# Gated experts on one Trainium2 core: the residual added into the accumulators at mid pass, and closing column products carried by ScalarE

## The chip, the cores and the metric

The kernel runs on one core of one Trainium2 chip. The metric is the device time of the whole program in microseconds, as the median of several runs. The profile is one further execution, taken by the hardware profiler; its span runs from the first to the last instruction. Engines are named TensorE (PE, its weight loads PEld), VectorE (DVE), ScalarE (ACT), GpSimd (POOL) and SyncE (SP, which issues nearly all DMAs; its queue is SPq).

## The reference

`x` is 8 blocks of 512 rows by 256 columns in fp32. Each block goes through eight experts and one shared expert. For an expert with weights Wg, Wu (256 x 1024) and Wd (1024 x 256):

```python
g = einsum('bsd,edf->ebsf', h, Wg)
u = einsum('bsd,edf->ebsf', h, Wu)
expert_outs = einsum('ebsf,efd->ebsd', silu(g) * u, Wd)
expert_output = einsum('be,ebsd->bsd', gating_probs, expert_outs)
shared = (silu(h @ Sg) * (h @ Su)) @ Sd
x = x + (1 - sg) * expert_output + sg * shared
```

The last line is the residual: the input `x` itself is added to the result. This sum is what the change moves.

## The kernel before

**Tiling.** The eight blocks are two halves of four (`h` = 0, 1, `NI` = 4). A half is worked through in 18 units: nine experts (the shared one is the ninth) times two groups of 512 of the 1024 hidden columns. Units are numbered 0 to 35; unit 17 is the last of the first half, unit 18 opens the second. In a unit, four blocks meet four weight tiles of 128 hidden columns. The kernel does not multiply each block with each tile in the plain way: it keeps combinations with the coefficients `CI` = (0, 1, -1, 2), which spares products. The four products of a block with its own tile make up the "hub" (P and Q steps), and the six pairs of blocks (`PAIRS`) follow, with differences and sums of inputs (`x_difference`, `x_sums`) and of weights (`w_difference`, `w_sums`). A pair has two steps R1 (a product of differences, L503) and four steps R (L513), for the gate (m = 0) and the up projection (m = 1). Gate results go through SiLU on ScalarE (L444), VectorE multiplies them with the up result and the expert's coefficient to h (L449).

**Down projection.** `down` (L550) is a generator of 26 steps, called "D": three for each of six pairs (r, then S or s, then a product with X at L618), four p steps with row sums and four q steps with column sums. The results are collected for the whole half in SBUF accumulators `acc["b", i]` and `acc["B", i]`, one of each for a block (and S and V for pairs). They are "turned": hidden direction across partitions, rows along the free direction. A step in `carried` (L584) first lets ScalarE copy the accumulator into a PSUM bank (L578), lets TensorE add its product there, and lets ScalarE copy the bank back (L587). A step with `single` (L592) starts an empty bank, and `put` adds it to the accumulator on VectorE (L566, L568, L570). The down projection uses two PSUM banks in turn. In the unit that closes a half (unit 17, and 34 for the second) S and V are also emptied into b and B, which adds VectorE operations.

**Order.** The main loop walks a written string of steps: "G" is a step of gate and up, "D" a step of down. A unit's D steps are late by eleven: the first eleven D of a unit finish the down projection of the unit before. TensorE and GpSimd keep the written order everywhere; ScalarE keeps it only in unit 0. VectorE, SyncE and, after unit 0, ScalarE are ordered by a planner, which takes what is ready by its own cost model, earlier written work first. Each engine executes its own order strictly.

**Turning back.** When the first half has closed, `turn_back` (L663) transposes each accumulator on VectorE (L669) in the D steps of unit 18, adds the residual (L670), which SyncE has loaded as 32-column squares of `x` (`load_back`, L659), and stores the result in four DMAs (L673). For the second half `end_step` transposes the accumulators (L689), writes them to DRAM, loads them back by rows (L707), and GpSimd adds them to rows of `x` (L711). Unit 35 itself multiplies straight into rows (`tail`, L720), and `store_rows` adds and stores (L729, L731).

**First unit.** In unit 0 the x differences and sums are computed (VectorE L288 and L302, ScalarE L290, GpSimd L303) and stored to DRAM; later units load them (L292 `v`, L309 `b`). The differences lie in a pool `v` of three buffers, the sums in a pool `b` of two.

Of the kernel before, what the change touches and what calls it, by code (L numbers as in the profile page):

```python
# [16 lines left out]
def kernel(  # L17
# [40 lines left out]
    P = 128  # L58
# [63 lines left out]
    back = {}  # L122
# [18 lines left out]
    def load_rows(pool, tag, b):  # L141
        rows = []
        for c in range(2):
            if pool is not xpool:
                t = pool.tile([P, 2, D], F32, tag=tag, name=f"xin{b}_{c}")
            elif c == 0:
                both = pool.tile([P, NT, D], F32, tag=tag, name=f"xin{b}")
            if pool is xpool:
                t = both[:, 2 * c : 2 * c + 2]
# [7 lines left out]
    def squares(a, b, q):  # L157

        return a[b].rearrange("s (k q d) -> q s k d", k=2, d=32)[q]
# [122 lines left out]
    def x_difference(u, p):  # L282

        i, j = PAIRS[p]
        v = vpool.tile([P, S], F32, tag="v", name=f"v{u.name}_{p}")
        if (u.h, p) not in scratch:
            d = CI[i] - CI[j]
            ve.tensor_sub(v, xhub[u.h, i][:, 0], xhub[u.h, j][:, 0])  # L288
# [261 lines left out]
    def down(u, acc):  # L550
# [81 lines left out]
        for what in (0, 1, 2, 3, 4, "p0", "q0", 5, "q1", "p1", "q2", "p2", "q3", "p3"):  # L632
# [7 lines left out]
            else:  # L640
                flush_sums(u, "cols", i)
                po, _ = single(("q", i), u.ad[i], u.cols[i])
                put(("B", i), po, 1.0)
                done[what] = po
# [6 lines left out]

    BACK = [(0, 1), (0, 0), (2, 1), (2, 0), (1, 1), (1, 0), (3, 1), (3, 0)]

    def load_back(h, i):

        if (h, i) not in back:
            xr = iopool.tile([P, S // 32, 2, 32], F32, tag="io", name=f"xr{h}_{i}")
            for q in range(4):
                nc.sync.dma_start(xr[ts(q, 32)], squares(x, NI * h + i, q))  # L659
            back[h, i] = xr  # L660
        return back[h, i]

    def turn_back(h, i, r):  # L663

        b = NI * h + i
        block = ends.pop((h, i, r))
        xr = load_back(h, i)
        t = zpool.tile([P, S], F32, tag="z", name=f"to{b}_{r}")
        ve.transpose(t, block)  # L669
        ve.tensor_add(xr[:, :, r], t.rearrange("p (c d) -> p c d", d=32), xr[:, :, r])  # L670
        if (i, 1 - r) not in BACK[BACK.index((i, r)):]:
            for q in range(4):
                nc.sync.dma_start(squares(out, b, q), xr[ts(q, 32)])  # L673
            if i in (0, 2):
                load_back(h, i + 1)
# [5 lines left out]
    end_stores = []  # L681

    def end_step(kind, i):

        b = NI * (NH - 1) + i
# [5 lines left out]
        elif kind == "store":  # L691
            to = end_rows[i] = dram.tile([S, D], F32, tag=f"end{i}", name=f"endrows{i}")
            at = to.rearrange("(c r t) d -> r t c d", r=32, t=NT)
            for r in range(2):
                for q in range(4):
                    end_stores.append((
# [3 lines left out]
        elif kind == "x":  # L700
            last_rows[i] = load_rows(xpool, "x", b)
        elif kind == "load":
            at = end_rows[i].rearrange("(p t) d -> p t d", t=NT)
            end_rows[i] = []
            for c in range(2):
                t = sumpool.tile([P, 2, D], F32, tag="sum", name=f"endin{i}_{c}")
                nc.sync.dma_start(t, at[:, 2 * c : 2 * c + 2])  # L707
                end_rows[i].append(t)
        else:
            for xr, t in zip(last_rows[i], end_rows[i]):  # L710
                gp.tensor_tensor(xr, xr, t, ALU.add)  # L711
# [13 lines left out]
    def store_rows(j, c):  # L725
        b = NI * (NH - 1) + j
        xr = last_rows[j][c]
# [12 lines left out]
    def gate_up(u, nxt):  # L740
# [19 lines left out]
        for kind, i, m in hub_steps(u):  # L760
# [6 lines left out]
            elif kind == "P":  # L767
                P_step(u, i, m)
                if u.n == 0 and m == 1 and i in (1, 3):
                    for p, make in ahead[:2] if i == 1 else ahead[2:]:  # L770
                        make(u, p)
# [8 lines left out]
        if u.n == 0:  # L780
            make_ad(u)
            for p in range(len(PAIRS)):
                d_forms(u, p)
        for p in range(len(PAIRS)):
# [13 lines left out]
            for m in range(2):  # L798
                if not last:
                    R1_step(u, p + 1, m)  # L800
                    if m == 0 and u.n == 0 and p and p + 1 < len(PAIRS):
                        sums(p + 1)
# [3 lines left out]
                for r in range(2):  # L806
                    R_step(u, p, m, r)
                    if m == 1 and r == 1:
# [3 lines left out]
                        if p + 2 < len(PAIRS) and u.n:  # L812
# [16 lines left out]
        7: (("turn", 0), ("store", 0)), 16: (("turn", 1), ("store", 1)), 18: (("x", 0),),  # L829
        20: (("turn", 2), ("store", 2), ("x", 1)), 22: (("load", 0), ("x", 2)),  # L830
        24: (("turn", 3), ("store", 3), ("x", 3)), 28: (("add", 0),), 30: (("load", 1),),
        34: (("add", 1),), 37: (("load", 2),), 40: (("add", 2),), 44: (("load", 3),),
        47: (("add", 3),),
# [7 lines left out]
    AHEAD_AT = (8, 11, 14, 17, 20)  # L841
    BACK_AT = (6,10,11,13,15,18,20,23)
# [22 lines left out]
    for u in units:  # L865
# [6 lines left out]
        for what in FIRST if u.n == 0 else LAST if nxt is None else ORDER:  # L872
            if what == "G":
                if nG == TAKE:
                    for _ in behind:
                        pass
                    if u.opens:
                        acc = {}
                    behind = down(u, acc) if nxt is not None else iter(())
# [24 lines left out]
            else:  # L904
# [54 lines left out]
```

## Time and profile before

| | |
|---|---|
| median of 3 runs | 2446.45 us (2445.05 to 2447.55) |
| the profiled execution | 2446.47 us |
| its span | 2444.7 us |
| TensorE busy | 2431.5 us, 99% |
| VectorE busy | 1928.9 us, 79% |
| ScalarE busy | 1239.4 us, 51% |
| GpSimd busy | 2080.0 us, 85% |
| granted TensorE clock, mean | 0.999 |
| DMA, mean | 106 GB/s |

A row of the profile gives line, engine and operation, what is written from what is read, sizes and count, then busy time and the mean duration in ns, then the idle time of the engine before such instructions and what ended it. In a timeline a row is a start and a duration in us, and in brackets the idle time before with its releaser. In a table by stretches each engine has its busy time in that stretch and the number of its instructions, followed by the granted TensorE clock, the DMA share and GB/s. One fp32 product of 128 x 128 by 512 columns is recorded as two matmul instructions.

### The profile page before, as it was taken

How to read it: one execution, taken by the hardware profiler on the slowest of the kernel's cores; microseconds unless marked ns; L12 is line 12 of the kernel's file. 1: busy time of each engine (PE TensorE's matmuls, PEld its weight loads, DVE VectorE, ACT ScalarE, POOL GpSimd, SP SyncE). 2: the span in 40 equal slices, each digit the busy share in tenths (PEclk: the TensorE clock that was granted, in tenths of full speed). 3: DMA queues.
4: the chain of work that ended last, by engine and by line, in shares of the span. 5: the costliest groups of instructions: out<-in, count | busy, mean ns of one | idle time of the engine just before them, and what ended most of it. 6: DMA issues, size and time to landing. Idle time of an engine off the chain costs nothing.

```text
span 2444.7 us, 22778 instructions
## 1 busy us (share of the span) xinstructions
PE 2431.5 (99%) x5736; PEld 1085.1 (44%) x5736; DVE 1928.9 (79%) x2870; ACT 1239.4 (51%) x2294; POOL 2080.0 (85%) x2313
## 2 busy tenths in 40 slices
PE   9999999999999999999999999999999999999999
PEld 4444444444444444444444444444444444444446
DVE  7778878777777877787987777777777777777795
ACT  5555554554555555555445555555555555555542
POOL 8988888898988989898878888888888888888872
PEclk9999999999999999999999999999999999999999
DMA  4333343343433333344353233323333333233245
GB/s 158 101 105 111 104 112 112 103 134 102 126 110 97 105 111 97 106 129 125 112 118 120 85 95 91 91 81 99 99 104 103 95 97 92 88 91 92 86 117 149
DMA packets 237841, 260.02 MB, mean 106 GB/s; under 512 B 80656, under 2 KB 173072, under 8 KB 237712
## 3 DMA queue, kind: packets, MB, share of 16 engines
q1 hardware_dynamic: 236880, 258.27, 35.9%
q8 instruction: 48, 0.79, 0.1%
q14 instruction: 81, 0.66, 0.1%
q10 hardware_dynamic: 832, 0.30, 0.0%
HBM read 240.69 MB, written 17.83 MB: 106 GB/s over the span
## 4 chain that ended last, share of the span: by engine, by line
PE 96%; POOL 1%; DVE 1%; DMA 1%; issue 0%; ACT 0%; SPq 0%; ACTq 0%; DVEq 0%; POOLq 0%
PE c L513 30%; PE c L503 15%; PE c L481 10%; PE c L458 10%; PE r L595 7%; PE r L618 7%; PE S L579 5%; PE b L579 5%; PE q L595 5%; PE s L595 2%; PE tail L720 1%; DMA sgt<-ondB_sharedgateprob_dram 0%; POOL wd L429 0%; POOL wb L396 0%; DVE h L449 0%
## 5 line engine op out<-in xcount | busy, mean ns | idle before, releaser
L513 PE MATMUL c<-b,wb 128*128 128x512 f32 x1728 | 848.1, 593 | 2.6 <-DMA b<-xs 1.9
L444 ACT ACTIVATE sg<-c 128x512 f32<-128x512 f32 x576 | 343.8, 597 | 595.0 <-DVE c L518 343.7
L449 DVE SCALAR_TENSOR_TENSOR h<-sg,coef,c 128x512 f32<-128x512 f32 x576 | 427.8, 743 | 235.6 <-PE c L513 128.3
L513 PEld LDWEIGHTS c<-b,wb 128*128 128x128 f32 x1728 | 328.3, 190 | 412.9 <-issue 390.0
L503 PE MATMUL c<-v,u 128*128 128x512 f32 x864 | 441.5, 593 | 1.9 <-ACT c L498 1.4
L540 POOL TENSOR_TENSOR rows<-rows,h 128x512 f32<-128x512 f32 x280 | 369.0, 1318 | 0.0
L508 DVE TENSOR_TENSOR c<-D,c 128x512 f32<-128x512 f32 x432 | 298.7, 692 | 81.1 <-ACT sg L444 61.4
L540 POOL TENSOR_TENSOR cols<-cols,h 128x512 f32<-128x512 f32 x280 | 357.7, 1277 | 0.0
L518 DVE TENSOR_TENSOR c<-c,D 128x512 f32<-128x512 f32 x432 | 298.6, 691 | 22.3 <-PE c L513 22.1
L396 POOL TENSOR_TENSOR wb<-u,wb 128x256 f32<-128x256 f32 x108 | 79.2, 733 | 237.3 <-ACT wb L394 237.3
L458 PE MATMUL c<-x,w 128*128 128x512 f32 x572 | 274.5, 592 | 0.0
L503 PEld LDWEIGHTS c<-v,u 128*128 128x128 f32 x864 | 163.0, 189 | 210.0 <-issue 163.9
L595 PE MATMUL r<-h,wd 128*128 128x512 f32 x420 | 215.4, 594 | 0.0
L618 PE MATMUL r<-X,ud 128*128 128x512 f32 x420 | 214.5, 592 | 0.0
L529 DVE TENSOR_TENSOR X<-h,h 128x512 f32<-128x512 f32 x210 | 206.1, 982 | 6.8
L481 PE MATMUL c<-x,at 128*128 128x512 f32 x432 | 209.4, 593 | 1.2 <-DVE P L474 0.7
L491 ACT COPY D<-c 128x512 f32<-128x512 f32 x284 | 165.8, 584 | 83.8 <-DVE h L449 83.8
L540 POOL TENSOR_TENSOR rows<-h,h 128x512 f32<-128x512 f32 x140 | 195.4, 1396 | 0.0
L540 POOL TENSOR_TENSOR cols<-h,h 128x512 f32<-128x512 f32 x140 | 181.0, 1293 | 0.0
L464 ACT COPY P<-c 128x512 f32<-128x512 f32 x216 | 126.6, 587 | 106.9 <-PE c L458 102.3
L458 PEld LDWEIGHTS c<-x,w 128*128 128x128 f32 x572 | 108.5, 190 | 135.9 <-issue 111.9
L578 ACT COPY S<-accS 128x512 f32<-128x512 f32 x132 | 77.9, 590 | 149.8 <-DVE accV L566 140.7
(108 smaller groups left out, 3472.5 us busy)
## 6 DMA issues: line engine op xcount, KB each, us to landing
b<-xs SPq DMA_DIRECT2D x210, 512.0 KB, 3.6
v<-xs SPq DMA_DIRECT2D x210, 256.0 KB, 2.6
wd<-in_L_cond_Wd_dram SPq DMA_DIRECT2D x32, 512.0 KB, 4.9
w<-in_L_cond_Wg_dram SPq DMA_DIRECT2D x127, 128.0 KB, 3.5
w<-in_L_cond_Wu_dram SPq DMA_DIRECT2D x127, 128.0 KB, 3.6
f<-xd SPq DMA_DIRECT2D x12, 512.0 KB, 3.6
xs<-f SPq DMA_DIRECT2D x18, 256.0 KB, 3.0
xin<-in_x_dram SPq DMA_DIRECT2D x16, 256.0 KB, 4.1
```

The lines of the kernel that those rows point to most:

```text
L444: nc.scalar.activation(s, bank, AF.Silu)
L449: ve.scalar_tensor_tensor(t, u.sg[i, j], coef[:, u.e, b : b + 1], bank, ALU.mult, ALU.mult)
L458: nc.tensor.matmul(bank, u.raw[i][:, m, 0], xhub[u.h, i][:, 0], start=True, stop=True)
L481: nc.tensor.matmul(bank, u.at[i][:, m], xhub[u.h, i][:, 1], start=False, stop=True, skip_group_check=True,)
L503: nc.tensor.matmul(bank, u.U[p][:, m], u.V[p], start=False, stop=True, skip_group_check=True)
L508: ve.tensor_sub(other, u.Ds[j, m], bank)
L513: nc.tensor.matmul(bank, u.W[p][:, r, m], u.VB[p][:, r], start=False, stop=True, skip_group_check=True,)
L518: ve.tensor_add(bank, bank, u.Ds[j, m])
L540: gp.tensor_tensor(sums[n], u.h_[n, n] if first else sums[n], u.h_[at], ALU.add)
L579: nc.tensor.matmul(po, w, b, start=not full, stop=True, skip_group_check=full)
L595: nc.tensor.matmul(po, w, b, start=True, stop=True)
L618: nc.tensor.matmul(A, u.Ud[p], u.X[p], start=False, stop=True, skip_group_check=True)
```

## The change

It has these parts.

1. **Residual at mid pass.** A new generator `residual` adds `x` to the accumulators `b` and `B` of the half on VectorE, with the coefficients that the turned combinations need. One operation is taken at each of the D steps 7, 13 and 19 of units 11 to 15 of a half. It reads the turned input tiles that lie in SBUF for the whole half.
2. **Turning back without a residual.** `turn_back` transposes straight into the output tile. The loads of `x` as squares (`load_back`) and the additions (L670) are gone. The four stores of a block are put into a list `outgoing`, and one is issued per G step. In the end of the second half the loads of `x` rows and GpSimd's additions are gone; rows of a block are loaded by one DMA into the x pool, and three of the four loads stand at G step 31, 38 and 45 where they stood at 30, 37 and 44.
3. **Closing q steps.** In a closing unit the q product is `carried`: copied in and out by ScalarE, where it was `single` with an addition on VectorE.
4. **First unit.** The x differences of pairs 3 and 4 lie in buffers of the pool `io` (two buffers, otherwise unused there). The sums of the second pair and the difference of the third are written after the hub, and the sums of a pair are made at the end of the pair two before it, as in the other units, where they were made one G step later.

```diff
     def x_difference(u, p):
 
         i, j = PAIRS[p]
-        v = vpool.tile([P, S], F32, tag="v", name=f"v{u.name}_{p}")
+        if u.n == 0 and p in (3, 4):
+            v = iopool.tile([P, 2, S], F32, tag="io", name=f"v{u.name}_{p}")[:, 0]
+        else:
+            v = vpool.tile([P, S], F32, tag="v", name=f"v{u.name}_{p}")
...
                 flush_sums(u, "cols", i)
-                po, _ = single(("q", i), u.ad[i], u.cols[i])
-                put(("B", i), po, 1.0)
-                done[what] = po
+                if closes(u):
+                    carried(("B", i), u.ad[i], u.cols[i])
+                else:
+                    po, _ = single(("q", i), u.ad[i], u.cols[i])
+                    put(("B", i), po, 1.0)
+                done[what] = True
...
+    def residual(acc, h):
+
+        for i in range(NI):
+            c, b, B = CI[i], acc["b", i], acc["B", i]
+            v, A = xhub[h, i][:, 0], xhub[h, i][:, 1]
+            for to, x_, s in ((b, v, 1.0), (b, A, c), (B, A, 1.0 + c * c), (B, v, c)):
+                if s == 1.0:
+                    ve.tensor_add(to, to, x_)
+                elif s == -1.0:
+                    ve.tensor_sub(to, to, x_)
+                elif s != 0.0:
+                    ve.scalar_tensor_tensor(to, x_, s, to, ALU.mult, ALU.add)
+                else:
+                    continue
+                yield
...
-    def turn_back(h, i, r):
-
-        b = NI * h + i
-        block = ends.pop((h, i, r))
-        xr = load_back(h, i)
-        t = zpool.tile([P, S], F32, tag="z", name=f"to{b}_{r}")
-        ve.transpose(t, block)
-        ve.tensor_add(xr[:, :, r], t.rearrange("p (c d) -> p c d", d=32), xr[:, :, r])
-        if (i, 1 - r) not in BACK[BACK.index((i, r)):]:
-            for q in range(4):
-                nc.sync.dma_start(squares(out, b, q), xr[ts(q, 32)])
-            if i in (0, 2):
-                load_back(h, i + 1)
+    def turn_back(h, i, r):
+
+        if i not in backs:
+            backs[i] = iopool.tile([P, S // 32, 2, 32], F32, tag="io", name=f"to{h}_{i}")
+        t = backs[i]
+        ve.transpose(t[:, :, r], ends.pop((h, i, r)).rearrange("p (c d) -> p c d", d=32))
+        if (i, 1 - r) not in BACK[BACK.index((i, r)):]:
+            del backs[i]
+            at = out[NI * h + i].rearrange("s (k q d) -> q s k d", k=2, d=32)
             for q in range(4):
+                outgoing.append((at[q], t[ts(q, 32)]))
...
-                    for p, make in ahead[:2] if i == 1 else ahead[2:]:
+                    for p, make in ahead[:2] if i == 1 else ahead[2:3]:
...
         if u.n == 0:
+            for p, make in ahead[3:]:
+                make(u, p)
             make_ad(u)
...
-                    if m == 0 and u.n == 0 and p and p + 1 < len(PAIRS):
-                        sums(p + 1)
...
-                        if p + 2 < len(PAIRS) and u.n:
+                        if p + 2 < len(PAIRS):
                             sums(p + 2)
...
-        7: (("turn", 0), ("store", 0)), 16: (("turn", 1), ("store", 1)), 18: (("x", 0),),
-        20: (("turn", 2), ("store", 2), ("x", 1)), 22: (("load", 0), ("x", 2)),
-        24: (("turn", 3), ("store", 3), ("x", 3)), 28: (("add", 0),), 30: (("load", 1),),
-        34: (("add", 1),), 37: (("load", 2),), 40: (("add", 2),), 44: (("load", 3),),
-        47: (("add", 3),),
+        7: (("turn", 0), ("store", 0)), 16: (("turn", 1), ("store", 1)),
+        20: (("turn", 2), ("store", 2)), 24: (("turn", 3), ("store", 3)),
+        22: (("load", 0),), 31: (("load", 1),), 38: (("load", 2),), 45: (("load", 3),),
...
+    REST_IN, REST_AT = range(11, 16), (7, 13, 19)
...
-                if final and nxt is not None and nG in (30, 36):
-                    load_back(u.h, (nG - 30) // 3)
...
-                    if end_stores:
-                        nc.sync.dma_start(*end_stores.pop(0))
+                if outgoing:
+                    nc.sync.dma_start(*outgoing.pop(0))
...
+                if nD in REST_AT and u.n % (len(units) // NH) in REST_IN:
+                    next(rest, None)
```

More of the change, by code (lines that the diff above doesn't have):

```diff
@@ L121 @@
     scratch = {}
-    back = {}
+    outgoing = []
     xhub = {}
@@ L143, in load_rows @@
         for c in range(2):
[L144 to L149, printed above, removed]
+            t = pool.tile([P, 2, D], F32, tag=tag, name=f"xin{b}_{c}")
             nc.sync.dma_start(
@@ L154, in load_rows @@
         return rows
-    def squares(a, b, q):
-        return a[b].rearrange("s (k q d) -> q s k d", k=2, d=32)[q]
     def load_turned(to, b):
@@ L650, in down @@
             yield
-    BACK = [(0, 1), (0, 0), (2, 1), (2, 0), (1, 1), (1, 0), (3, 1), (3, 0)]
-    def load_back(h, i):
-        if (h, i) not in back:
-            xr = iopool.tile([P, S // 32, 2, 32], F32, tag="io", name=f"xr{h}_{i}")
-            for q in range(4):
-                nc.sync.dma_start(xr[ts(q, 32)], squares(x, NI * h + i, q))
-            back[h, i] = xr
-        return back[h, i]
-    def turn_back(h, i, r):
-        b = NI * h + i
-        block = ends.pop((h, i, r))
-        xr = load_back(h, i)
-        t = zpool.tile([P, S], F32, tag="z", name=f"to{b}_{r}")
-        ve.transpose(t, block)
-        ve.tensor_add(xr[:, :, r], t.rearrange("p (c d) -> p c d", d=32), xr[:, :, r])
-        if (i, 1 - r) not in BACK[BACK.index((i, r)):]:
-            for q in range(4):
-                nc.sync.dma_start(squares(out, b, q), xr[ts(q, 32)])
-            if i in (0, 2):
-                load_back(h, i + 1)
+    def residual(acc, h):
[12 more added lines that the diff above has]
+                yield
+    BACK = [(0, 1), (0, 0), (2, 1), (2, 0), (1, 1), (1, 0), (3, 1), (3, 0)]
+    backs = {}
+    def turn_back(h, i, r):
[6 more added lines that the diff above has]
+            at = out[NI * h + i].rearrange("s (k q d) -> q s k d", k=2, d=32)
+            for q in range(4):
+                outgoing.append((at[q], t[ts(q, 32)]))
     last_rows = {}
@@ L680 @@
     end_rows = {}
-    end_stores = []
     def end_step(kind, i):
-        b = NI * (NH - 1) + i
         if kind == "turn":
@@ L695, in end_step @@
                 for q in range(4):
-                    end_stores.append((
+                    outgoing.append((
                         at[:, :, :, ts(4 * r + q, 32)],
@@ L699, in end_step @@
                     ))
-        elif kind == "x":
-            last_rows[i] = load_rows(xpool, "x", b)
-        elif kind == "load":
+        else:
             at = end_rows[i].rearrange("(p t) d -> p t d", t=NT)
[L704 to L711, printed above, removed]
+            last_rows[i] = xpool.tile([P, NT, D], F32, tag="x", name=f"endin{i}")
+            nc.sync.dma_start(last_rows[i], at)
     def tail(u, i, j, c):
@@ L726, in store_rows @@
         b = NI * (NH - 1) + j
-        xr = last_rows[j][c]
+        xr = last_rows[j][:, 2 * c : 2 * c + 2]
         for t in (0, 1) if j == NI - 1 and c == 1 else (slice(0, 2),):
@@ L878 @@
                         acc = {}
+                        rest = residual(acc, u.h)
                     behind = down(u, acc) if nxt is not None else iter(())
```

## The prediction

> **What bounds the kernel now.** I read the page's busy shares first, then busy time by stretch, then the timelines around the stretches in which TensorE is not full.
>
> ```profile
> PE 2431.5 (99%) x5736; PEld 1085.1 (44%) x5736; DVE 1928.9 (79%) x2870; ACT 1239.4 (51%) x2294; POOL 2080.0 (85%) x2313
> ```
>
> ```profile
> core 0: us, PE busy (x) PEld busy (x) DVE busy (x) ACT busy (x) POOL busy (x), PEclk, DMA share, GB/s
> 18.00:68.00 50.00, 46.83 (x106) 19.03 (x105) 42.84 (x60) 25.21 (x50) 49.30 (x55) 1.00 0.36 122
> 68.00:1180.00 1112.00, 1112.00 (x2592) 492.00 (x2591) 876.61 (x1302) 576.57 (x1065) 984.43 (x1091) 1.00 0.37 111
> 1180.00:1240.00 60.00, 58.63 (x134) 24.67 (x133) 58.42 (x92) 26.67 (x49) 52.16 (x59) 1.00 0.26 77
> 1240.00:1270.00 30.00, 27.57 (x60) 11.45 (x59) 25.28 (x37) 13.97 (x27) 14.56 (x15) 0.94 0.73 154
> 1270.00:2330.00 1060.00, 1060.00 (x2472) 469.08 (x2471) 830.51 (x1234) 548.55 (x1014) 915.76 (x1019) 1.00 0.33 96
> 2330.00:2382.00 52.00, 50.82 (x117) 21.47 (x116) 51.45 (x82) 22.41 (x41) 39.96 (x38) 1.00 0.37 100
> ```
>
> The bound is TensorE. In the two long stretches it has no idle time, and the change alters no product, so only the four short ones can be won: the first unit, the close of the first half, the opening of the second, the close of the second. In both closes VectorE is as full as TensorE (58.42 of 60, 51.45 of 52). Undisturbed, one 512-column product follows the next after 0.86 us; what a step is longer is lost. Summed so, about 5 us go in the first unit, 2.8 and 4.8 at the half boundary, 2.5 in the last close.
>
> First unit, timeline of four engines:
>
> ```profile
> 38.02 1.26 POOL L303 TENSOR_TENSOR b<-v,x 128x512 f32<-128x512 f32 x1
> 39.32 1.20 DVE L288 TENSOR_TENSOR v<-x,x 128x512 f32<-128x512 f32 x1 [2.61 <-POOL b L303]
> 44.80 0.59 ACT L498 COPY c<-f 128x512 f32<-128x512 f32 x1 [5.93 <-DVE h L449]
> 45.44 1.13 PE L503 MATMUL c<-v,u 128*128 128x512 f32 x2 [1.35 <-ACT c L498]
> 67.24 1.12 PE L513 MATMUL c<-b,wb 128*128 128x512 f32 x2 [0.64 <-POOL wb L396]
> ```
>
> The sixth x difference needs the third one's buffer (three in the pool), which GpSimd's L303 reads until 39.28. VectorE stands 2.61 us, its next h, the seed copy and the product follow late.
>
> Half boundary, timelines of SyncE and TensorE:
>
> ```profile
> 1252.05 0.57 SPq L673 DMA_DIRECT2D out_dram<-xr  x1
> 1252.81 3.00 SPq L659 DMA_DIRECT2D xr<-in_x_dram  x4
> 1255.86 2.53 SPq L673 DMA_DIRECT2D out_dram<-xr  x3
> 1258.49 0.62 SPq L309 DMA_DIRECT2D b<-xs  x1
> 1262.98 1.79 PE L513 MATMUL c<-b,wb 128*128 128x512 f32 x2 [1.91 <-DMA b<-xs]
> 1264.56 1.91 PE L595 MATMUL r<-h,wd 128*128 128x512 f32 x2
> ```
>
> The load of b is issued behind four stores and four residual loads and lands 4.36 us later (chain of work). Then products last twice as long: the clock is 0.94 over these 30 us.
>
> **What the Trainium skill says.** "TensorE: Matmul & The Clock Gate", Part 1: after an idle window of about 3.4 us the clock is halved; here a wait of some 2 us was followed by about 3.4 us at half clock, so the trace is stricter. "SBUF — State Buffer", Who interferes with whom: a VectorE instruction with two SBUF inputs contends with a GpSimd one that reads SBUF. The trace agrees: additions of that kind take 0.69 to 1.7 us (rows below and L302), those with one PSUM operand 0.69. "VectorE: DVE Perf Modes", The TRN2 errata: fp32 tensor_tensor takes (N+151)/0.96, 691 ns for 512, which is the uncontended 0.69.
>
> **The change part by part.** Against the profiled execution's 2446.47 us (span 2444.7 and 1.8 around it; the median of the runs shown is 2446.45, so the sum carries over).
>
> ```profile
> L529 DVE TENSOR_TENSOR X<-h,h 128x512 f32<-128x512 f32 x210 | 206.1, 982 | 6.8
> L670 DVE TENSOR_TENSOR xr<-to,xr 128x512 f32<-128x512 f32 x8 | 7.2, 924 | 0.0
> 793.78 0.75 DVE L449 SCALAR_TENSOR_TENSOR h<-sg,coef,c 128x512 f32<-128x512 f32 x1 [1.84 <-PE c L513]
> 1217.35 0.68 DVE L568 TENSOR_TENSOR accb<-accb,r 128x512 f32<-128x512 f32 x1
> 1218.15 0.59 ACT L464 COPY P<-c 128x512 f32<-128x512 f32 x1 [0.27 <-PE c L458]
> ```
>
> *Residual at mid pass.* Coefficients 0, 1, -1, 2 give 2+4+4+4 = 14 VectorE operations a half, 28 in all. All operands lie in SBUF, so I price them like L529: 28 x 0.98 = 27.4 us (19 uncontended, 47 at the worst L302's 1.68). They stand at steps D7, D13, D19 of units 11 to 15. D13 and D19 are steps with the S product, after which VectorE waits for TensorE: 1.84 us before 793.78, a gap of that kind in every pair, longer than 0.98. After D7 the free stretches are shorter (0.3, 0.2, then 1.66 us at 765.2), but the additions behind have about 2 us before their products. So 0 on TensorE; without the gap it would be up to 0.98 each. No acc is read until the next unit's copy, except acc b1 at one D7, whose operation must follow that step's copy back. Bounds: 0 to +3.
>
> *Residual out of the turning.* Eight L670 go (7.4 us of VectorE, at 1234 to 1276), sixteen xr loads with issues of 0.75 us each (12 us of SyncE's queue), and the stores leave one per G instead of four in a row. (a) b load: its buffer is free when the second pair's last product ends, near 1250.5. With even four stores ahead at 0.7 it is issued by 1254.2 and lands 4.4 later, 1258.6, before the product needs it at 1260.8. So the whole loss goes: 1259.97 to 1267.32 is 7.35 us for four products (3.43), 3.92, and 0.22 before it: -4.1. (b) The wait at 1251.95 (L503 for a ScalarE seed behind VectorE's c, with two L670 in the 6 us before): 1.49 - 0.86 and 0.07 after: -0.7. (c) The 0.28 at 1237.46, a p product whose bank VectorE frees late; one L670 and one q addition (0.6 pitch each) leave that chain: -0.3. What is late next is the transposes, waiting for one of two io buffers; their stores would have to be 2 us late to matter.
>
> *Closing q products on ScalarE.* Eight (four a close): VectorE loses 8 x 0.687 = 5.5 us, ScalarE gains a copy in (0.595) and out (0.590) each, 9.5 us of a 51% engine. The copy in now stands before the product. For q0 the bank is the one that L568 reads until 1218.03; ScalarE takes its P copy (1218.15, pitch 0.48) first, then copies to about 1219.22, and the product planned at 1218.81 starts near 1219.27: +0.45 and 0.1 for the late weight. The second close has the same order (L568 to 2363.93, P copy 2364.05, q at 2364.71): again +0.55. Sum +1.1; if ScalarE takes q first 0.4 each less; at worst, with P and the f behind it late, 1.1 each. q1 to q3 have 0.9 us or more. The relief of VectorE takes the waits at 2379.3 and 2380.7 (0.08 + 0.25): -0.3.
>
> *First unit.* The fourth and fifth x difference take io buffers, so the sixth takes the first one's, free since the second pair. The 2.61 go; TensorE gets back 43.06 to 45.44 (2.38 - 0.86) and 0.10 behind: -1.6. Sums one step earlier: in GpSimd's written order wb of the third pair no longer stands behind w difference L384 (0.7), so the wait before 41.27 (0.25 + 0.08) goes: -0.3. The last pair's sums pass an addition (1.72) and an at (1.18); the loss at 67.24, 0.79 + 0.10, goes: -0.9, unless three operations of the next unit are still put before it. The waits at 18.9 and 26.2 (0.9 and 1.0) come from f and P of the hub; the moved b and v operations filled gaps there and I give them no gain (bounds -1.5 to +0.5).
>
> *The end.* GpSimd's eight additions (10.0 us) and eight x loads go, eight row loads become four of 512 KB; they hang behind nothing TensorE waits for after 2382. From its last product to the end nothing changes. 0.
>
> Sum: -4.1 - 0.7 - 0.3 + 1.1 - 0.3 - 1.6 - 0.3 - 0.9 = -7.1. That is 2437.6 for the span and **2439.3 us**.
>
> **Rivals.** *SyncE's queue stays in the way* (16 in 100): the planner orders SyncE and VectorE by its own costs, and if it puts stores before b whose transposes come late, the b wait stays, its cause only renamed; also where (a) goes but two of the smaller gains fail. For it: the store at 1252.05 did wait for VectorE. Against: no loads, and fewer stores in a row. Gain 7.1 - 4.1 = 3.0: 2443.4.
> *More than counted* (14): the hub waits of the first unit go too, and ScalarE takes q first: -7.1 - 1.5 - 0.9 = -9.5: 2436.9.
> *Slower* (8): each residual operation lands not in the gap but in the run before h and the seed copy, where the seed ends about 0.4 us before its product (798.24 and 798.66). Then each costs up to 0.6, 28 x 0.6 = 16.8, net +9.7: 2456. From 0.25 an operation on the gain is eaten, from 0.43 it is slower by over 0.2%. Against: it needs nearly all 28, while the first half's input preparation puts VectorE transposes into the same stretches with no TensorE idle.
> That it does nothing is excluded only for the removed issues; with the b wait moved and the first unit's chain unchanged it would be near 2446, inside the first rival.
>
> **How the numbers follow.** Forecast 62, rivals 16, 14, 8. Within 0.2% (4.9 us, about what a measurement can tell from no change) lies the first rival and 6 of the forecast's 62, where small gains fail: same 0.22. Faster 56 + 14 = 0.70. Slower 0.08. The range runs from 2436.0 (more than counted, its bound) to 2444.0 (first rival with a little more lost).
>
> **What would show it.** No TensorE wait on b at the boundary, clock 1.00 there; no 2.61 us wait before L288; a seeded q0 product some 0.5 us late in both closes; the long stretches still with no idle time beside 28 additions; the 2 us of waits for S copies in each close unchanged. Wrong, if a TensorE wait appears between 700 and 1180, or if b or a transpose's buffer is late behind the stores.

## The result, and the profile after

The changed kernel takes 2449.2 us (median of 22 executions, 2447.7 to 2453.24) beside 2446.61 us for the kernel before on the same chip (22 executions, 2444.98 to 2448.09): ratio 1.0014, 95% interval 1.0008 to 1.0020, so 2 to 5 us slower. The forecast was 2439.3 us, with a range of 2436 to 2444. The waits at the half boundary went as forecast; the residual at its new place took more than that gave, and the first unit lost where a gain was forecast.

The profiled execution of the changed kernel took 2450.91 us (span 2448.9). The page's first part, busy time by engine:

```profile
PE 2433.2 (99%) x5736; PEld 1084.3 (44%) x5736; DVE 1944.9 (79%) x2882; ACT 1247.4 (51%) x2310; POOL 2077.0 (85%) x2305
```

VectorE has 16 us more than before and twelve instructions more, ScalarE 8 us more (14.5 and 9.5 follow from the prediction's durations). Busy time by stretch (columns: stretch and its length, then the engines, granted clock, DMA share, GB/s):

```profile
core 0: us, PE busy (x) PEld busy (x) DVE busy (x) ACT busy (x) POOL busy (x), PEclk, DMA share, GB/s
18.00:68.00 50.00, 46.99 (x102) 18.93 (x102) 43.02 (x58) 23.91 (x49) 46.40 (x54) 0.97 0.38 129
68.00:1180.00 1112.00, 1109.75 (x2583) 489.81 (x2582) 885.80 (x1313) 574.66 (x1063) 987.36 (x1090) 1.00 0.36 108
1180.00:1240.00 60.00, 58.53 (x135) 25.00 (x134) 57.74 (x91) 28.16 (x53) 51.04 (x56) 1.00 0.39 107
1240.00:1270.00 30.00, 29.93 (x70) 13.04 (x70) 22.82 (x34) 18.93 (x37) 20.88 (x25) 1.00 0.52 114
1270.00:2330.00 1060.00, 1057.65 (x2463) 467.27 (x2462) 838.36 (x1241) 547.19 (x1012) 914.73 (x1014) 1.00 0.33 96
2330.00:2382.00 52.00, 50.51 (x116) 21.38 (x115) 50.69 (x79) 24.28 (x45) 41.93 (x40) 1.00 0.33 87
```

Three differences from before. The opening of the second half (1240 to 1270) is full, 29.93 instead of 27.57, at clock 1.00. The two long stretches, full before, now lack 2.25 and 2.35 us. The first unit ran at clock 0.97.

Here and below, "by steps" is a sum: for each matmul record of 512 columns, what its start lies later than 0.43 us after the start of the one ahead of it. This includes the weight load that is late after a wait, and products at half clock. From 17 us on it is 15.5 us before and 20.0 after; the difference of 4.5 is about that of the spans (4.2).

| stretch | before | after | forecast of the difference |
|---|---|---|---|
| first unit, 17 to 68 us | 5.2 | 6.7 | -2.8 |
| 68 to 1180 | 0 | 3.8 | 0 |
| close of the first half | 2.9 | 3.0 | +0.25 (+0.55 and -0.3) |
| opening of the second half | 4.8 | 0 | -4.8 |
| 1270 to 2330 | 0 | 3.4 | 0 |
| second close | 2.5 | 3.1 | +0.25 (+0.55 and -0.3) |

In the rows below, c is a PSUM bank of a gate or up product, b and wb are the input and weight sums that an R step multiplies, P and f are copies and differences of the hub's results. A seed is ScalarE's copy into a bank, to which a product then adds.

**First unit**, timelines of VectorE and TensorE after:

```profile
21.44 2.91 DVE L282 TENSOR_TENSOR v<-x,x 128x512 f32<-128x512 f32 x2
24.28 0.73 DVE L443 SCALAR_TENSOR_TENSOR h<-sg,coef,c 128x512 f32<-128x512 f32 x1
24.93 3.66 DVE L468 TENSOR_TENSOR P<-P,c 128x512 f32<-128x512 f32 x6
26.86 3.81 PE L475 MATMUL c<-x,at 128*128 128x512 f32 x4 [2.31 <-DVE P L468]
```

The waits on the sixth difference (before: 2.61 us ahead of L288) and on the sums wb near 41 and 67 are gone, as forecast. But the fourth and fifth difference, whose buffers are now free from the start, stand ahead of the hub's h and six subtractions. The hub's product at 26.86 waits for these subtractions 2.31 us, and then two products take 3.81 us instead of 1.88: half clock, as the Trainium skill's "TensorE: Matmul & The Clock Gate", Part 1, describes, but after a wait of 2.3 us, where the page has an idle window of about 3.4.

**Residual**, its costliest group on VectorE, then timelines of VectorE, ScalarE and TensorE:

```profile
L656 DVE TENSOR_TENSOR accb<-accb,x 128x512 f32<-128x512 f32 x10 | 9.9, 991 | 1.2 <-ACT accb L581 0.9
```

```profile
976.69 1.17 DVE L656 TENSOR_TENSOR accb<-accb,x 128x512 f32<-128x512 f32 x1
977.78 1.75 DVE L523 TENSOR_TENSOR X<-h,h 128x512 f32<-128x512 f32 x1
979.45 1.75 DVE L660 SCALAR_TENSOR_TENSOR accb<-x,accb 128x512 f32<-128x512 f32 x1
981.13 0.68 DVE L502 TENSOR_TENSOR c<-D,c 128x512 f32<-128x512 f32 x1
984.00 0.61 ACT L492 COPY c<-f 128x512 f32<-128x512 f32 x1
984.71 1.10 PE L497 MATMUL c<-v,u 128*128 128x512 f32 x2 [1.13 <-issue]
...
1029.37 1.50 DVE L660 SCALAR_TENSOR_TENSOR accB<-x,accB 128x512 f32<-128x512 f32 x1
1030.79 2.46 DVE L468 TENSOR_TENSOR P<-P,c 128x512 f32<-128x512 f32 x4
1032.72 0.70 PE L475 MATMUL c<-x,at 128*128 128x512 f32 x1 [0.56 <-DVE P L468]
```

The duration was priced well: 30.0 us for the 28 instead of 27.4. The place was not. Beside e2 below, where each stands at its written step, they come up to 60 us early (the seventh at 836.68 instead of 896.61); the planner did not put them at the step that the program names. Six places cost TensorE time: two additions around an X at 976 to 981, three operations of 4.67 us in a row ahead of the work on c, so that the seed at 984.00 and its product come late (1.7 us by steps); one addition straight ahead of the hub's subtractions at 960.28 (0.41) and at 1029.37 (0.83); in the second half the same at 2171, 2190 and 2240 (0.8, 1.7, 0.8). Together 3.0 and 3.4 us. The others cost nothing.

**Half boundary**, timelines of SyncE and TensorE:

```profile
1248.48 1.28 SPq L879 DMA_DIRECT2D out_dram<-to  x2
1255.80 0.33 SPq L303 DMA_DIRECT2D b<-xs  x1
1256.64 0.58 SPq L879 DMA_DIRECT2D out_dram<-to  x1
1265.04 1.02 PE L507 MATMUL c<-b,wb 128*128 128x512 f32 x2
```

The load of b is issued at 1255.80, as soon as its buffer is free: the two stores ahead of it have long been issued, where before four stores and four loads stood in between. The first product that reads it starts at 1265.04 without waiting.

**Closing column product**, timelines of ScalarE and TensorE:

```profile
1223.13 0.59 ACT L458 COPY P<-c 128x512 f32<-128x512 f32 x1 [0.27 <-PE c L452]
1223.61 0.60 ACT L572 COPY B<-accB 128x512 f32<-128x512 f32 x1
1224.26 1.12 PE L573 MATMUL B<-cols,wd 128*128 128x512 f32 x2 [0.31 <-ACT B L572]
```

ScalarE takes the P copy first, as worked out, then the seed; with the weight load that comes late after the wait, q0 (the first of the four q products) loses 0.58 us in each close (0.55 forecast). Behind the last one, q3, a wait of 0.33 by steps is new.

### The profile page after: what moved, and what is told of

Same layout as the page of the kernel before. It is cut to its first block, busy times and chain, and to the rows that moved or that the text cites. A ratio compares the mean times of both kernels' runs of the same rounds, so it can differ in the third digit from the quotient of the medians.

```text
span 2448.9 us, 22750 instructions
## 1 busy us (share of the span) xinstructions
PE 2433.2 (99%) x5736; PEld 1084.3 (44%) x5736; DVE 1944.9 (79%) x2882; ACT 1247.4 (51%) x2310; POOL 2077.0 (85%) x2305
## 4 chain that ended last, share of the span: by engine, by line
PE 96%; DVE 3%; POOL 0%; ACT 0%; DMA 0%; issue 0%; DVEq 0%; POOLq 0%; ACTq 0%; SPq 0%
PE c L507 29%; PE c L497 14%; PE c L475 10%; PE c L452 9%; PE r L589 7%; PE r L612 7%; PE b L573 5%; PE S L573 5%; PE q L589 4%; PE s L589 2%; PE tail L713 1%; DVE h L443 0%; DVE P L468 0%; DVE X L523 0%; DMA b<-xs 0%
```

## The experiments

Each ratio is to the kernel before, run beside it on the same chip, with its 95% interval. Lines of kernels with an edit are shifted by up to a few from those above.

| run | what is in it | us | before | ratio |
|---|---|---|---|---|
| e1 | changed, no residual | 2442.72 | 2445.91 | 0.9988 (0.9982 to 0.9995) |
| e2 | changed, residual at its written place | 2447.07 | 2445.91 | 1.0005 (0.9996 to 1.0013) |
| e3 | changed, residual in the gap | 2442.99 | 2445.91 | 0.9989 (0.9981 to 0.9997) |
| e4 | changed, two differences later | 2448.72 | 2445.91 | 1.0012 (1.0005 to 1.0018) |
| e5 | changed, closing products as before | 2447.88 | 2445.81 | 1.0010 (1.0003 to 1.0016) |
| e6 | before, with the io buffers alone | 2447.96 | 2445.81 | 1.0008 (1.0002 to 1.0015) |
| e7 | changed, repairs of e3, e4, e5 | 2441.39 | 2445.81 | 0.9981 (0.9974 to 0.9988) |
| e8 | e7, three sums later | 2442.31 | 2445.81 | 0.9986 (0.9979 to 0.9992) |
| e9 | changed, stores in a row | 2451.71 | 2445.98 | 1.0026 (1.0017 to 1.0036) |
| e10 | changed, without the io buffers | 2449.92 | 2445.98 | 1.0016 (1.0010 to 1.0023) |
| e11 | e7, two x sums on VectorE | 2439.32 | 2445.98 | 0.9971 (0.9961 to 0.9982) |
| e12 | changed, without residual, io buffers and carried q products | 2441.96 | 2445.98 | 0.9982 (0.9975 to 0.9990) |

**e1: is it the residual?**

```diff
-                if s == 1.0:
-                    ve.tensor_add(to, to, x_)
...
+                if s == 0.0:
                     continue
                 yield
```

> The changed kernel without its 28 residual additions in mid pass; its output therefore lacks the x term, and no other work takes their place. Theory R (the residual costs TensorE time, 0 was wrong): the long stretches 68-1180 and 1270-2330 lose under 0.5 us each instead of 2.25 and 2.35 by the windows (3.8 and 3.4 by start-to-start steps), and so do the late hub products; 2442 to 2443.5 us, 6 to 7 below the changed kernel. Rival N (the loss in the long stretches comes from elsewhere in the change, for instance from another placing of GpSimd's sums): the stretches keep over 2 us each and the time stays within 1.5 us of 2449.

2442.72 us. Against the changed kernel's 1.0014 the ratio falls by 0.0026, 6.4 us; the direct losses by steps were 3.0 + 3.4. Busy time by stretch of e1:

```profile
68.00:1180.00 1112.00, 1111.54 (x2591) 491.80 (x2590) 876.91 (x1304) 575.56 (x1065) 984.49 (x1091) 1.00 0.36 109
1270.00:2330.00 1060.00, 1059.44 (x2469) 468.66 (x2468) 828.68 (x1235) 547.85 (x1012) 912.40 (x1016) 1.00 0.32 95
```

In the second stretch no product waits before 2325; the 0.56 is the first wait of the close, which has moved into it. In the first one product at 645.43 waits 0.46. So the residual costs all of 6.4 us. Rival N falls.

**e2 and e3: its presence or its place?** e2 holds each addition at its place in the program's order:

```diff
-                    ve.tensor_add(to, to, x_)
+                    made = ve.tensor_add(to, to, x_)
...
+                tc.keep_in_program_order(made)
```

> The changed kernel with each residual addition held at the place in VectorE's order at which the program writes it (the step's place), so that none is moved ahead of earlier work. Theory P (what counts is which instruction stands right behind it): the 18 to 20 operations of steps D13 and D19 then stand between the subtraction and the addition into the c banks, ahead of the h on which TensorE's down products hang, where the chain has some 0.35 us to spare; each costs 0.3 to 0.9, so 6 to 18 us in place of the 6 to 7 of the changed kernel: 2449 to 2460 us, with the waits now at c<-c,D and h instead of at the six subtractions. Rival M (the moving ahead is the fault, the written place is harmless, as the prediction held): 2442 to 2443.5 us. Rival B (any 28 such operations cost about the same, through the contention with GpSimd): within 1 us of 2449.

e3 puts those of D13 and D19 behind the pair's last addition into c, so into VectorE's wait ahead of h, and holds those of D7 at their written place:

```diff
-            ve.tensor_add(bank, bank, u.Ds[j, m])
+            u.last_c = ve.tensor_add(bank, bank, u.Ds[j, m]).ins
...
+                behind_c = at_d[0] != 7
+                with tc.issue_after(at_u[0].last_c) if behind_c else ExitStack():
```

> The changed kernel with the residual additions of steps D13 and D19 held behind the pair's last addition into a c bank (so they fall into VectorE's 1.84 us wait ahead of h), and those of D7 at their written place. Theory P (the place decides): the loss in the long stretches falls to under 1 us in each half, and the time to 2442 to 2444 us although all 28 operations are there. Rival B (the operations cost wherever they stand, since they share SBUF with GpSimd): at least 4 us of the loss stays, 2446.5 us or more.

e3 takes 2442.99 us, as if the residual were not there (e1: 2442.72). All 28 operations run, 28.3 us by their groups. Timeline of VectorE and busy time by stretch of e3:

```profile
793.25 0.68 DVE L662 TENSOR_TENSOR accb<-accb,x 128x512 f32<-128x512 f32 x1
795.18 0.75 DVE L443 SCALAR_TENSOR_TENSOR h<-sg,coef,c 128x512 f32<-128x512 f32 x1 [1.25 <-PE c L507]
```

```profile
68.00:1180.00 1112.00, 1111.47 (x2590) 491.55 (x2589) 887.29 (x1316) 575.60 (x1065) 990.10 (x1092) 1.00 0.36 109
1270.00:2330.00 1060.00, 1059.44 (x2469) 468.65 (x2469) 840.15 (x1248) 547.28 (x1012) 916.38 (x1016) 1.00 0.33 96
```

The addition sits in the gap that the prediction pointed at, and VectorE still waits 1.25 us after it. Theory P holds, B falls.

e2, at 2447.07, lies between. Timelines of VectorE, ScalarE and TensorE of e2:

```profile
779.02 0.68 DVE L656 TENSOR_TENSOR accB<-accB,x 128x512 f32<-128x512 f32 x1
779.63 0.69 DVE L512 TENSOR_TENSOR c<-c,D 128x512 f32<-128x512 f32 x1
780.83 0.73 DVE L443 SCALAR_TENSOR_TENSOR h<-sg,coef,c 128x512 f32<-128x512 f32 x1
782.01 0.59 ACT L492 COPY c<-f 128x512 f32<-128x512 f32 x1
782.65 1.12 PE L497 MATMUL c<-v,u 128*128 128x512 f32 x2
```

The written place of D13 and D19 is not the gap but between the two operations on c, ahead of the next h and the seed copy: the prediction's slower rival, at its place. It costs 0.24 us for each of the 18 (0.13 of waiting and 0.10 for the late weight load), 4.3 us; the ratios of e2 and e1 differ by 0.0017, 4.2 us. I had expected 0.3 to 0.9 each.

**e4: the hub of the first unit.**

```diff
-            ve.tensor_sub(v, xhub[u.h, i][:, 0], xhub[u.h, j][:, 0])
+            with tc.issue_after(u.last_h) if p in (3, 4) else ExitStack():
+                ve.tensor_sub(v, xhub[u.h, i][:, 0], xhub[u.h, j][:, 0])
```

> The changed kernel with the fourth and fifth x difference of the first unit held behind the last h of its hub; nothing else is altered. Theory F (with their buffers free from the start the two subtractions, 1.24 and 1.75 us, are put ahead of the six P-c subtractions that the hub's fourth product waits for): the wait of 2.3 us ahead of the product at 26.86 and the 3.4 us at half clock behind it go, the first unit loses 2.4 to 3.5 us instead of 6.7, and the time is 2444.8 to 2446 us, 3.3 to 4.3 below the changed kernel. Rival G (the hub's delay is of GpSimd's or ScalarE's making): the wait stays, and the time is within 1 us of 2449. Rival H (the late differences delay the third or fourth pair instead): a wait of over 1 us appears between 33 and 60, and the gain is under 2 us.

2448.72 us: nothing that the intervals can tell from the changed kernel. The hub's wait is gone in the profile (its fourth product follows without a pause at 23.5), so G falls. But timelines of TensorE and GpSimd of e4:

```profile
65.43 1.12 PE L508 MATMUL c<-b,wb 128*128 128x512 f32 x2 [1.98 <-POOL wb L391]
64.20 1.17 POOL L391 TENSOR_TENSOR wb<-u,wb 128x256 f32<-128x256 f32 x1
```

Of the 2.5 us won in the hub 2.2 are lost 40 us later, at the last wb. From 26 us on GpSimd works without a pause (49.30 of the 50 us from 18 to 68, the same 49.30 as before the change). H is right in kind, but the wait lies from 63 to 65 us, behind the stretch that I gave.

**e6 and e10: the io buffers alone, and taken back.** e6 adds to the kernel before:

```diff
+        if u.n == 0 and p in (3, 4):
+            v = iopool.tile([P, 2, S], F32, tag="io", name=f"v{u.name}_{p}")[:, 0]
+        else:
+            v = vpool.tile([P, S], F32, tag="v", name=f"v{u.name}_{p}")
```

> The kernel before with one part of the change: the first unit's fourth and fifth x difference in io buffers. Prediction's step: the first unit loses 2.8 us less, 2443 us beside 2446. Theory F (two subtractions without a buffer to wait for are put ahead of the hub's six): a wait of about 2 us ahead of the hub's fourth product, a loss of 4.2 to 6.7 us in the first unit in place of 5.2 (the upper end where a stretch at half clock follows), so from 1 us faster to 1.5 slower than before; and the waits on VectorE's 2.61 us and on wb near 41 and 67 gone, as predicted.

e10 takes them from the changed kernel (the edit shown with e12 below). The sums stay where the change moved them, in e10 as in e12; moved alone they were not run.

> The changed kernel with the first unit as before (fourth and fifth x difference back in the pool of three). Prediction's step: 2.8 us slower than the changed kernel, since VectorE's 2.61 us wait comes back. Theory F (the io buffers only let two subtractions ahead of the hub's six; GpSimd bounds the unit anyway): faster than the changed kernel by 1 to 2.5 us, as e6 was 2.0 us slower than before by its ratio; the hub's fourth product waits about 0.7 us instead of 2.3 and the stretch at half clock is gone.

e6, the kernel before with these lines, is slower by 0.0008 (0.5 to 3.7 us). Its TensorE:

```profile
26.56 1.12 PE L484 MATMUL c<-x,at 128*128 128x512 f32 x2 [2.33 <-DVE P L477]
```

The wait is that of the changed kernel, without the residual and without the rest. VectorE's wait for the buffer is gone, but the one on wb at 67 us stays (0.8 by steps), against the expectation. The executions of e6 at full clock take 2446.25 us by the median, those of the kernel before 2445.67; 15 of 21 have a mean clock below 1.000, and only 9 of 68 of the kernel before. By these medians about 0.6 us are waits, and the rest comes with more frequent half clock. e10, the changed kernel without these lines, has the old waits again, VectorE's on the buffer included:

```profile
24.86 1.12 PE L475 MATMUL c<-x,at 128*128 128x512 f32 x2 [0.67 <-DVE P L468]
38.90 1.20 DVE L282 TENSOR_TENSOR v<-x,x 128x512 f32<-128x512 f32 x1 [3.25 <-POOL b L297]
45.70 1.12 PE L497 MATMUL c<-v,u 128*128 128x512 f32 x2 [2.03 <-ACT c L492]
```

and 1.0016 beside 1.0014: neither the 2.8 us slower of the prediction nor the 1 to 2.5 faster of theory F. Its first unit loses 6.0 us by steps beside the 5.2 of before: with the sums moved, VectorE's wait on the buffer is 3.25 us instead of 2.61. The buffers trade one wait of 2 us for another. What they cost by themselves lies between nothing and some 2 us and is not settled closer.

**e5: the closing products.**

```diff
-                if closes(u):
-                    carried(("B", i), u.ad[i], u.cols[i])
-                else:
-                    po, _ = single(("q", i), u.ad[i], u.cols[i])
-                    put(("B", i), po, 1.0)
+                po, _ = single(("q", i), u.ad[i], u.cols[i])
+                put(("B", i), po, 1.0)
```

> The changed kernel with the closing column products written as before: a product into an empty bank, added to the accumulator by VectorE. Prediction's step (the seed's copy stands before the product: +0.55 a close for q0, at most 0.3 given back by VectorE's relief): q0 is on time again in both closes (0.58 each by the changed kernel's steps), and the time falls by 0.5 to 1.1 us. From the trace of the changed kernel one adds 0.33 a close behind q3, which was not predicted: then the fall is 1.2 to 1.8 us, less 0.3 to 0.7 if the waits at the last product of the hub and at a p product come back. Rival (the carried form is as good or better, because VectorE is the fuller engine in the closes): no change or up to 1 us slower than the changed kernel.

1.0010, so 1.0 us below the changed kernel by the ratios, within the intervals of no difference. The steps are clear: q0's 0.58 is gone in both closes. The 0.33 behind q3 (the product at 1240.90 of the changed kernel, and again in the second close) is exchanged for 0.33 of the old kind, at the hub's last products and q3. So VectorE's relief, forecast at -0.3, bought nothing in the second close, and the part costs 1.15 us by steps.

**e12 and e9: the half boundary.** e12 leaves the residual out altogether, with closing products and difference buffers as before (the edits of e1 and e5, and this one):

```diff
-        if u.n == 0 and p in (3, 4):
+        if False:
             v = iopool.tile([P, 2, S], F32, tag="io", name=f"v{u.name}_{p}")[:, 0]
```

> The kernel before with the turning back stripped of the residual (no loads of x there, no additions, one store per step) and nothing in its place: closing products and first unit as before, the residual left out, so the output lacks the x term. Prediction's steps: boundary -4.1 -0.7 and close -0.3, so 5.1 us below before, all of it at 1240 to 1270 us and 0.3 at 1237. Theory C (of the 4.8 us that the profiled execution of before loses there, about 1.9 is a stretch at half clock that only some executions have): 3 us below before, by the median.

2441.96 us, 0.9982: 4.4 us below before (2.4 to 6.1). Busy time by stretch of e12:

```profile
1180.00:1240.00 60.00, 58.83 (x136) 24.98 (x135) 57.58 (x92) 27.04 (x50) 50.88 (x58) 1.00 0.33 93
1240.00:1270.00 30.00, 30.00 (x72) 13.26 (x71) 26.28 (x38) 16.91 (x33) 20.04 (x22) 1.00 0.55 125
```

The boundary is whole, and 0.4 us by steps are won in the close. The interval holds both the prediction's 5.1 and theory C's 3. C is right on one point: in e6, which has the old boundary, the stretch has no half clock and loses 2.6 us by steps, not 4.8. The half clock is an event of some executions: only 9 of the 68 executions of before beside e5 to e8 have a mean clock below 1.000, and they take 2447.85 us by the median, the others 2445.67. The profiled execution from which I priced the boundary was one of the few. Since e12 lacks three parts of the change, their single effects can be added to it: -4.4, the residual +6.4 (e1), the closing products +1.0 (e5), the io buffers -0.5 (e10) to +2.0 (e6), together +2.5 to +5.0 beside the measured +3.4.

e9 asks whether the loads or the row of stores held b back:

```diff
-                if outgoing:
+                while outgoing:
                     nc.sync.dma_start(*outgoing.pop(0))
```

> The changed kernel with the four stores of a finished block issued in a row, as before the change; the sixteen loads stay away. Prediction's step (a): even with four stores ahead, at 0.7 us each, the load of b is issued in time, so the stretch from 1240 to 1270 us stays within 0.5 us of full and the time within 0.8 us of the changed kernel (ratio to the kernel before 1.0011 to 1.0018). Rival (it was the run of stores, each waiting for its transpose, that held b back, not the loads): TensorE waits for b again, 1.5 to 2.5 us, and the time rises by as much.

2451.71 us, some 2.9 more than the changed kernel, yet not at the boundary. Busy time by stretch, SyncE and TensorE of e9:

```profile
1240.00:1270.00 30.00, 30.00 (x72) 13.25 (x71) 22.90 (x35) 18.06 (x35) 20.24 (x23) 1.00 0.49 115
```

```profile
2400.30 5.28 SPq L879 DMA_DIRECT2D endrows<-end  x8
2405.68 0.56 SPq L303 DMA_DIRECT2D b<-xs  x1
2410.03 1.10 PE L507 MATMUL c<-b,wb 128*128 128x512 f32 x2 [1.71 <-DMA b<-xs]
```

At the boundary b is on time, but step (a)'s four stores did not stand in its way: the first block's were issued by 1250.2, before the buffer of the next b was free (1253.8), and the second block's only from 1263.51 on, behind the b after it. The edit also put the last unit's eight stores of a block in a row, which wait for their transpose until 2400.30 and need 5.28 us to issue; there b comes late, and TensorE loses 2.5 us. So the rival's mechanism exists, with eight stores directly ahead of b; four were not tried there. An estimate from the trace of before: without the 3.0 us of loads b would have been issued near 1255.5 and have landed 4.36 us later, at 1259.9, ahead of its product at 1260.8. The change took both out of the way, and which of them would have been enough alone is not shown.

**e7, e8, e11: the repairs together.** e7 has the edits of e3, e4 and e5.

> The changed kernel with three repairs: residual additions in the gap ahead of h, the first unit's two differences behind the hub's last h, the closing column products as before. If the single effects add: e3 gave about 6 us, e4 0.3 (in the profile 0.9 leaving out the half clock), the closing products 0.5 to 1.5, so 7 to 8 us below the changed kernel, 3.5 to 5 below the kernel before: 2441 to 2442.5. Theory W (the first unit is bound by GpSimd, so what its hub no longer loses is lost before the next unit's first product): the wait of about 2 us on wb near 63 us stays.

2441.39 us: as expected, and a wait on the last wb stays (1.0 us, 1.3 by steps, where about 2 were expected). e8 leaves three sums of h to the second unit:

```diff
-                if nG > TAKE and nG % 2 == 0 and u.sums:
+                if nG > TAKE and nG % 2 == 0 and u.sums and (u.n or nG not in (30, 34, 38)):
```

> As e7, and three of the first unit's sums of h (GpSimd, 1.27 us each) left to the second unit. Theory W (GpSimd's order bounds the first unit: in e4 it works without a pause from 27 to 72 us and delivers the last wb 2 us late): the wait on wb near 63 us goes, TensorE's loss in the first unit falls to about 2 us, and the time is 1.5 to 2.3 us below e7: 2439 to 2440.5. Rival X (the second unit's GpSimd work is as tight): the wait moves to between 70 and 130 us, and the gain over e7 is under 0.7 us.

2442.31 us, no gain over e7. The wait near 64 us goes, and comes back in the second unit, as rival X has it:

```profile
87.71 1.13 PE L590 MATMUL q<-cols,ad 128*128 128x512 f32 x2 [2.20 <-POOL cols L535]
```

e11 takes work from GpSimd instead of moving it in time:

```diff
-            gp.tensor_tensor(b[:, 1], v, xhub[u.h, i][:, 1], ALU.add)
+            if u.n == 0 and p in (3, 4):
+                ve.tensor_add(b[:, 1], v, xhub[u.h, i][:, 1])
+            else:
+                gp.tensor_tensor(b[:, 1], v, xhub[u.h, i][:, 1], ALU.add)
```

> As e7, and two of the first unit's x sums (1.27 to 1.7 us of GpSimd each) on VectorE, which has some 7 us of its own idle there. Theory W (GpSimd's queue bounds the first unit): the last wb comes 2.5 to 3.4 us earlier, the wait of 1.2 us ahead of the product near 64.8 us goes, nothing returns at 85 to 95 us, and the time is 0.8 to 1.5 us below e7: 2440 to 2440.6 beside 2445.8 before. Rival V (VectorE cannot take them without delaying c, h and seeds): a wait of 0.5 to 1.5 us appears between 40 and 60 us and the time is that of e7 or above.

2439.32 us, 0.9971: 4 to 10 us below the kernel before, and the lowest median here, though from 7 executions and with an interval that overlaps e7's. It is below what was expected: none of its executions has half clock, and beside e7's at full clock (2440.59) 1.3 us remain. No wait on wb is left and none comes back at 85 to 95 us; one of 0.53 us by steps, on a seed copy at 55.8, is what rival V foresaw. That GpSimd's work sets the wait at the end of the first unit is shown by the traces of e4, e8 and e11 together: the wait follows that work wherever it is put, and goes where it is taken away.

## Why the prediction was wrong

*Residual at mid pass, 0.* This step failed, and it alone turns the sign: 6.4 us. The prediction said "They stand at steps D7, D13, D19", and of D13 and D19 that VectorE "waits for TensorE" there. The number (28), the duration (30.0 us against 27.4) and the gap were right; e3 shows that in the gap they are free. But the step in the program is not the place in VectorE's order: the planner put most of them earlier, where 4.67 us of VectorE in a row cost 1.7, and one addition ahead of the hub's subtractions 0.4 to 0.8. Nor is the written place the gap (e2). The bound of +3 took the delay of single operations, not of a row of three.

*First unit, -2.8.* Failed. Each wait named did go, but a buffer that comes free earlier is also an order that changes: the two subtractions went ahead of the hub (+2.5 and, in the profiled execution, 1.9 at half clock, where e6 at full clock still loses 0.9). I had given the moved operations "no gain" and a bound of -1.5 to +0.5; the loss was above it. Behind that stands GpSimd: with 49.30 of 50 us busy in the view that the prediction itself showed, the unit's end was GpSimd's, and a wait of TensorE taken away in it comes back at the next wb (e4).

*Half boundary, -4.1 and -0.7.* Right by steps: 4.8 became 0, and b is issued as soon as its buffer is free. That four stores directly ahead of it would do no harm, as (a) has it, was not tested. Mis-sized as a part of the median: some 1.7 of the 4.8 was a stretch at half clock (1262.98 to 1266.9 in the steps), which few executions of before have.

*Closes, +1.1 and -0.3.* q0 was right to 0.03 us, with its cause. (c), -0.3 at 1237, came. The relief of VectorE, -0.3, was replaced by as much behind q3.

*The end, 0.* Right: from TensorE's last product to the last instruction 3.78 us before, 3.73 after.

*The slower rival* had the right cause in the wrong place: residual operations ahead of what TensorE awaits, in a few places at up to 1.7 us, not at nearly all 28 at 0.6. Taken at its own place (e2) it costs 0.24.

Open: one load of b each near 647 and 856 us makes a product wait 0.3 to 0.4 in the changed kernel (0.9 at most in other runs; e6, with its old residual, has such waits too), and none in the profiled execution of before; it was not studied.

## What to carry to other kernels

Ask of every instruction that a change adds or sets free not at which step the program names it, but behind which other it will stand on its engine, and who waits for that one; where a planner orders the engine, hold it behind the last instruction before a known gap. A wait on TensorE may only be counted as won if no other engine is full over the same stretch: here GpSimd's queue returned 2 us, 40 us later. And look at whether a half-clock stretch in the profiled execution is in the other executions too, before it is priced as part of the kernel.

## What was not expected of the hardware

A wait of TensorE of some 2 us is followed by half clock in some executions and in others of the same kernel not. The changed kernel has a mean clock below 1.000 in 10 of 22 executions, median 2451.56 us, the others 2448.34; e4, e6 and e7, with single waits of 1.0 to 2.3 us, have it in 9, 15 and 6 of 21, 21 and 16; e11, whose longest wait in the first unit is 0.67 us, in none of 7. In the traces the waits of 2.33 (e6) and 1.98 us (e4) were followed by full speed, that of 2.31 us (changed kernel) by half.

The record of the granted clock in the traces shows a pattern. Four have a stretch at half clock ahead of the last product (before, changed, e3, e12). Each lasts 3.41 us, and each begins a whole number of 3.413 us after the record's first entry: 368, 6, 6 and 12 times. So does, in all 14 traces, the half clock that follows the last product. If time is divided into windows of that length from there, the idle time of TensorE within one window tells the cases apart. Busy time by window, changed kernel, then e6:

```profile
23.66:27.07 3.41, 1.10 (x4) 0.27 (x3) 3.41 (x6) 0.00 (x0) 3.33 (x6) 1.00 0.74 297
27.07:30.48 3.41, 3.41 (x4) 0.96 (x4) 3.41 (x6) 1.07 (x2) 3.25 (x7) 0.50 0.42 165
```

```profile
22.73:26.14 3.41, 1.51 (x4) 0.38 (x2) 3.41 (x5) 0.26 (x1) 3.41 (x5) 1.00 0.53 214
26.14:29.55 3.41, 2.32 (x5) 0.97 (x6) 3.41 (x7) 1.10 (x3) 3.18 (x7) 1.00 0.82 324
```

The changed kernel's wait lies within one window, 2.31 us idle of 3.41; the longer wait of e6 falls across two, and the first has 1.90. The windows ahead of the four stretches had 1.97 to 2.31 us idle; the idlest ones that full clock followed had 1.98 (e4), 1.93 (e10) and 1.90 (e6). So a limit near 2 us within one window fits all the traces, except that e4 and the kernel before (1.97) lie too close together to tell. Where the windows lie against the work differs: the first entry comes 4.0 to 7.1 us into the span. For the executions without a trace none of this is recorded.

The same VectorE addition of two SBUF operands took from 0.67 to 1.75 us here (the 28 of the changed kernel). That it contends with GpSimd is what the Trainium skill's "SBUF — State Buffer", Who interferes with whom, leads to expect; but short ones run beside a busy GpSimd too (0.67 us at 920.55). What tells is the GpSimd instruction that is running when the addition starts. For the addition at 979.45, which took 1.75 us:

```profile
978.94 1.71 POOL L534 TENSOR_TENSOR cols<-h,h 128x512 f32<-128x512 f32 x1
```

It has 1.20 us left, and the addition ends 0.55 later. In all 28 the duration is what that instruction has left plus 0.55 us, to within 0.08, and at least 0.67; the same holds for all 210 subtractions X<-h,h of the kernel before. So where three long ones meet in a row the mean of 1.0 us says little.
